# A selective-scan layer with a feed-forward network: ScalarE's side work moved behind the two decay exponentials of each group, and one exponential of the carried state issued two groups later

## The chip, the core and the metric

The kernel runs on one core of a Trainium2 chip. A core has five engines that work side by side, each through its own queue in order: TensorE (PE, matrix products, with PEld for its weight loads), VectorE (DVE), ScalarE (ACT), GpSimd (POOL) and SyncE (SP, which here only starts DMAs). An instruction that needs another engine's result waits on a semaphore, and everything behind it in its queue waits with it. The metric is the device time of one execution in microseconds (us); the three timed runs of the kernel before took 2914.01, 2914.90 and 2921.65 us, median 2914.9.

## What is computed

The input x is 2 sequences of 1024 tokens with 512 channels. The layer is a selective state-space model, a residual and a layer norm, then a gated feed-forward network, a residual and a layer norm:

```python
xn = x * rsqrt(mean(x*x) + 1e-6) * norm_w
xn = xn * sigmoid((xn @ select_proj_w.T + select_proj_b) * select_gate)
delta, B, C = split(xn @ x_proj_w.T)              # 128 + 128 + 128
dt = softplus(delta @ dt_proj_w.T + dt_proj_b)    # 512 channels
A = -exp(A_log)                                   # 512 x 128
h = exp(dt * A) * h + (dt * xn) * B               # per token: 512 x 128 states
y = sum over the 128 states of h * C
x = layernorm(x + (y + x * D) @ out_proj_w.T)
x = layernorm(x + (silu(x @ w_gate.T) * (x @ w_up.T)) @ w_down.T)   # 512 -> 2048 -> 512
```

The recurrence over tokens is the large part: 512 x 128 states for each of 2048 tokens.

## The kernel before

**Blocks, halves and groups.** The 2048 tokens are cut into 64 blocks of S = 32 tokens (`st`). A block is done in two halves (`h`, with `i` = 0 or 1), a half in eight groups (`r` = 0 to 7), so there are 1024 groups (`k`), 16 in a block. In this text the groups of a block are numbered 0 to 15; groups 0 to 7 have `i` = 0. A group covers 32 channels x 32 tokens with the 128 states on the partitions, and is one scan on VectorE over 1024 columns (L730): `h = a * h + bu`.

**The main path of a group.** TensorE makes `bu` = B (dt x) for the group with two matrix products (L709), and `a` = A dt for the *next* group with two more (L418). ScalarE turns those two into the decay factors `a_sb` with two exponentials (`decay_exp`, L425); this document calls the two the *pair* of the group. `a` has two buffers, so the next group's `a` products can only start when this group's pair has been read; `bu` has two buffers as well, and `a_sb` three. The state carried over from the previous block is added to the first column of `bu`: in even groups by VectorE (L727, from `cd`), in odd ones by a ScalarE copy of a sum made beforehand (L717, from `cu`). Groups 1, 5, 9 and 13 also run 16 products of the previous half's `h` with C (`y_round`, L437; the profile shows each product as two records, so 32).

**The carried state.** For each block, `load` fetches the first token's dt into all partitions (`cd`), the u rows (`cu`) and b0. At the end of group 5, `carry_a` for the next block issues three operations: ScalarE scales `cu` (L361), POOL multiplies `cd` by A (L362), and ScalarE takes the exponential of that product (L363). After group 9 of the same block, and after group 1 of the next, `carry_h` multiplies the result by the last states on POOL (L375, L376).

**The side work.** Everything else is written as Python generators that the class `Work` steps while the groups are issued: `pre` (norm, gate, projections, dt and u of the next 128 or 256 tokens), `post` (out projection, residual, norm), `ffn` and `silu`. A generator yields "E" when its next step is work for the other engines, "P" when it next wants TensorE and the one PSUM bank of the side work, and "H" while it holds that bank with products still to issue. `Work.others` steps each generator that stands at "E" once. `Work.tensor` issues one unit of products for the holder. `PARTS = (3, 0, 2, 3, 3, 0, 2, 3)` is what each group of a half adds to the credit of units; in groups with 0 no side products are issued.

**The order within a group, as issued:** first `others()` (L689, all side operations), then in group 0 `load` for the next block and in group 8 `y_out` of the previous block (ScalarE copies the finished `y` out of PSUM, L450, three POOL operations follow, L451 to L453), then the four products, the odd groups' copy (L717), the first exponential of the pair, VectorE's addition (L727), the second exponential, the scan, the C h products, the side products, `diag` (POOL builds the diagonal operands `ddt` and `du` of later groups, L389 and L399), and at last the carry operations. The order of calls is the order in each engine's queue.

**One chain of side work matters below.** A pair of feed-forward hidden tiles goes: products `gu` (L553) -> ScalarE copies them out (L561) -> POOL clamps and multiplies (L593, L594) -> ScalarE exp and ln (L596, L597) -> ScalarE exp (L599) -> POOL product into `hid` (L601). Four such pairs make half of `hid`; then the products `d` (L575) over its eight columns run, one unit for each column. Each arrow over "E" costs one call of `others()`. After `d`, VectorE adds the result to the row (L581).

Of the kernel before, what the change touches and what calls it, by code (L numbers as in the profile page):

```python
# [10 lines left out]
AF = mybir.ActivationFunctionType  # L11
# [10 lines left out]
PARTS = (3, 0, 2, 3, 3, 0, 2, 3)  # L22
# [12 lines left out]
def kernel(  # L35
# [17 lines left out]
    nc = tc.nc  # L53
# [11 lines left out]
    NSB = L // S  # L65
    NS = B * NSB
# [265 lines left out]
    prepared, carried, dus, ddts, hs, ys = {}, {}, {}, {}, {}, {}  # L332

    def load(st):


        ub = step_pool.tile([P, 2, P], FP, tag="ub", name=f"ub_{st}")
        nc.sync.dma_start(ub, ub_d[st].rearrange("g t b c -> (g t) b c"))
        prepared[st] = ub
        nc.gpsimd.tensor_copy(  # L340
            cz[st % 3][:, 28:284].rearrange("p (b w) -> p b w", w=32)[:, :, 0:4],
            made[lot_of[st]][1][:, toks(st)].rearrange("p (b t) -> p b t", t=4),
        )
        if st % NSB:
            cd = step_pool.tile([P, D], FP, tag="cd", name=f"cd_{st}")
            nc.sync.dma_start(cd, dt0_d[st : st + 1, :].to_broadcast([P, D]))
            cu = step_pool.tile([P, 2, P], FP, tag="cu", name=f"cu_{st}")
            for g in range(2):
                nc.sync.dma_start(
                    cu[:, g, :], ub_d[st, 2 + g, 0:1, 0, :].to_broadcast([P, P])  # L350
                )
            b0 = step_pool.tile([P, 1], FP, tag="b0", name=f"b0_{st}")
            nc.sync.dma_start(b0, ub_d[st, 0, 0, 1, :].unsqueeze(1))
            carried[st] = cd, cu, b0

    def carry_a(st):

        if st % NSB == 0:
            return
        cd, cu, b0 = carried[st]  # L360
        nc.scalar.activation(cu, cu, AF.Copy, scale=b0)  # L361
        nc.gpsimd.tensor_tensor(cd, a_n, cd, ALU.mult)  # L362
        nc.scalar.activation(cd, cd, AF.Exp, scale=-1.0)  # L363

    def carry_h(st, i):

# [41 lines left out]
    def place(k):  # L408
        h, r = divmod(k, 8)
        m, pair = divmod(r, 2)  # L410
        return h, m, pair

    def decay_mm(k, b):

        h, m, pair = place(k)
        g = 2 * pair + b
        ps = ps_a.tile([P, 16, S], FP, tag="a", name=f"a_{k}_{b}")
        nc.tensor.matmul(  # L418
            ps, a_t[ts(g, 32), m, :], ddts[k // 4][ts(g, 32), m % 2, :, :],
            start=True, stop=True,  # L420
        )
        return ps

    def decay_exp(k, b, ps):
        nc.scalar.activation(  # L425
            a_sb[:, k % 3, ts(b, 16), 1:], ps[:, :, 1:], AF.Exp, scale=-1.0
        )
# [16 lines left out]
    def y_out(st):  # L444

        tt, s = divmod(st, 4)
        if s == 0:
            yrs[tt] = post_pool.tile([P, 4, P], FP, tag="yr", name=f"yr_{tt}")
        yc = post_pool.tile([P, P, 4], FP, tag="yc", name=f"yc_{st}")
        nc.scalar.copy(yc, ys.pop(st).rearrange("p (q t) -> p q t", t=4))  # L450
        nc.gpsimd.tensor_tensor(yc, yc, pick.unsqueeze(1).to_broadcast([P, P, 4]), ALU.mult)  # L451
        nc.gpsimd.tensor_tensor(yc[:, :, 0:2], yc[:, :, 0:2], yc[:, :, 2:4], ALU.add)
        nc.gpsimd.tensor_tensor(yrs[tt][:, s, :], yc[:, :, 0], yc[:, :, 1], ALU.add)  # L453
        if s == 3:
            work.add(post(tt), front=True)
# [3 lines left out]
    def post(tt):  # L459

        zT = post_pool.tile([P, NM, P], FP, tag="zT", name=f"zT_{tt}")
        nc.sync.dma_start(zT, x_q.rearrange("(m p) t -> p m t", p=P)[:, :, ts(tt, P)])
        yield "E"
        yield "E"
        nc.gpsimd.tensor_tensor(zT, zT, dq.unsqueeze(2).to_broadcast([P, NM, P]), ALU.mult)
        yield "E"
        yield "P"
        ps = misc(f"zT_{tt}", 2)
        for s in range(4):
            nc.tensor.transpose(ps[:, ts(s, P)], yrs[tt][:, s, :], ident)  # L470
            if s == 1:
                yield "H"
        yield "E"
        z = zT.rearrange("p m (s t) -> p s m t", t=S)
        nc.vector.tensor_tensor(
            z, z, ps.rearrange("p (s m t) -> p s m t", m=NM, t=S), ALU.add
        )
        x1 = post_pool.tile([P, D], FP, tag="x1", name=f"x1_{tt}", bufs=4)
        nc.sync.dma_start(x1, xf[tt])
        yield "P"  # L480
        ps = misc(f"op_{tt}", 8)
        for half in (slice(0, 256), slice(256, 512)):
            for k in range(NM):
                nc.tensor.matmul(  # L484
                    ps[:, half], zT[:, k, :], out_w[:, k, half], start=(k == 0), stop=(k == NM - 1)
                )
                yield "H" if half.start == 0 or k + 1 < NM else "E"
        nc.vector.tensor_tensor(x1, x1, ps, ALU.add)
        yield "E"
        yield from normalize(x1, f"a{tt}")  # L490
        work.add(ffn(tt, x1))
# [129 lines left out]
    class Work:  # L621
# [11 lines left out]
        def step(self, item):  # L633
# [2 lines left out]
                self.gens.remove(item)  # L636
            item[1] = kind

        def others(self):
            for item in list(self.gens):  # L640
                if item[1] == "E":
                    if self.holder is item:
                        self.holder = None
                    self.step(item)
# [22 lines left out]
    work = Work()  # L667
# [17 lines left out]
    for k in range(NG):  # L685
        h, m, pair = place(k)
        st, i = divmod(h, 2)
        r = k % 8
        work.others()  # L689
        if r == 0:  # L690
            hs[h] = half_pool.tile([P, 256, S], FP, tag="h", name=f"h_{h}")

            if i == 1 and st:
                y_out(st - 1)
            if i == 0:
                c = lot_of[st]
                if c + 1 < NC and c not in begun:
                    begun.add(c)
                    pres[c + 1] = work.add(pre(c + 1), front=True)
                if st + 1 < NS:  # L700
                    if lot_of[st + 1] > c:
                        work.finish(pres[c + 1])
                    load(st + 1)

        bu = ps_bu.tile([P, 32, S], FP, tag="bu", name=f"bu_{k}")
        nxt = []
        for b in range(2):
            g = 2 * pair + b
            nc.tensor.matmul(  # L709
                bu[:, ts(b, 16), :], prepared[st][ts(g, 32), 1, :],  # L710
                dus[k // 4][ts(g, 32), m % 2, :, :],
                start=True, stop=True,
            )
            if k + 1 < NG:
                nxt.append(decay_mm(k + 1, b))
        if st % NSB and pair:
            nc.scalar.copy(  # L717
                bu[:, :, 0].rearrange("p (g e) -> p g e", e=16),
                carried[st][1][:, :, ts(2 * m + i, 16)],
            )  # L720
        if nxt:
            decay_exp(k + 1, 0, nxt[0])
        if st % NSB and not pair:
            left = carried[st][0].rearrange("p (b i e) -> p b i e", i=2, e=16)
            first = bu[:, :, 0].rearrange("p (b e) -> p b e", e=16)
            at = 4 * m + 2 * pair
            nc.vector.tensor_tensor(first, first, left[:, at : at + 2, i, :], ALU.add)  # L727
        if nxt:
            decay_exp(k + 1, 1, nxt[1])
        nc.vector.tensor_tensor_scan(  # L730
            hs[h][:, ts(r, 32), :].rearrange("p q t -> p (q t)"),
            a_sb[:, k % 3, :, :].rearrange("p q t -> p (q t)"),
            bu.rearrange("p q t -> p (q t)"),
            0.0, ALU.mult, ALU.add,
        )
        if h:
            for b in ROUNDS[r]:
                y_round(h - 1, b)
        credit = min(credit + PARTS[r], 6)
        done, most = 0, min(credit, 4)  # L740
        while PARTS[r] and (done < most or done < 4 and work.left == 1):

            if done == 3 and work.left == 2:
                break
            if not work.tensor():
                break
            done += 1
        credit -= done

        j, r4 = divmod(k, 4)  # L750
        if r4 == 3:
            diag(j + 2, 0)
        else:
            diag(j + 1, r4 + 1)
        if r == 1:
            if i == 0 and st:
                carry_h(st, 1)
            if i == 1 and st + 1 < NS:
                carry_h(st + 1, 0)
        if r == 5 and i == 0 and st + 1 < NS:  # L760
            carry_a(st + 1)
    for j in range(8):
        y_round(2 * NS - 1, j)
    y_out(NS - 1)
# [79 lines left out]
```

## Time and profile before

| | before |
|---|---|
| median of 3 runs | 2914.9 us |
| the profiled execution, whole | 2915.46 us |
| its span | 2913.5 us |
| PE busy | 2814.4 us |
| DVE busy | 2459.7 us (the 1024 scans: 2315.0) |
| POOL busy | 1837.0 us |
| ACT busy | 1640.5 us (the 2048 decay exponentials: 1084.1) |
| mean granted TensorE clock | 0.977 |
| first scan starts / last one ends | 43.7 / 2843.8 us |

Busy time is the union of an engine's records. A TensorE record begins when the product enters the array's queue, so a stretch in which the products wait on a semaphore is partly shown as busy, and a busy PE is not a PE at its peak. "Idle before" in the tables is the engine's idle time just before an instruction, and the arrow names what ended it. "PEclk" is the granted share of the TensorE clock. Of the whole time, about 41 us lie before the first group and 72 us behind the last one, where the last 128 tokens go through the feed-forward network alone; the 1024 groups between them take 2800 us, 2.73 us each.

### The profile page before, as it was taken

How to read it: one execution, taken by the hardware profiler on the slowest of the kernel's cores; microseconds unless marked ns; L12 is line 12 of the kernel's file. 1: busy time of each engine (PE TensorE's matmuls, PEld its weight loads, DVE VectorE, ACT ScalarE, POOL GpSimd, SP SyncE). 2: the span in 40 equal slices, each digit the busy share in tenths (PEclk: the TensorE clock that was granted, in tenths of full speed). 3: DMA queues.
4: the chain of work that ended last, by engine and by line, in shares of the span. 5: the costliest groups of instructions: out<-in, count | busy, mean ns of one | idle time of the engine just before them, and what ended most of it. 6: DMA issues, size and time to landing. Idle time of an engine off the chain costs nothing.

```text
span 2913.5 us, 58135 instructions
## 1 busy us (share of the span) xinstructions
PE 2814.4 (97%) x22728; PEld 1541.5 (53%) x22728; DVE 2459.7 (84%) x1680; ACT 1640.5 (56%) x3663; POOL 1837.0 (63%) x2140
## 2 busy tenths in 40 slices
PE   7989999999999999999999999999999999999998
PEld 4435555555555554555545555555555555455557
DVE  2998898888888988888888888989888898888881
ACT  4656566555565556655556555655556555455552
POOL 4656676666676666666567666566576666566653
PEclk6999999999999999999999999999999999999999
DMA  2011331323223331323313332133322323222325
GB/s 75 23 30 66 97 100 55 120 93 111 73 76 111 98 119 56 93 94 106 118 58 88 101 112 94 65 99 103 113 92 73 106 81 123 92 88 84 109 88 181
DMA packets 139166, 266.86 MB, mean 92 GB/s; under 512 B 22480, under 2 KB 76240, under 8 KB 138896
## 3 DMA queue, kind: packets, MB, share of 16 engines
q1 hardware_dynamic: 138896, 263.16, 28.1%
q8 instruction: 182, 2.98, 0.4%
q14 instruction: 88, 0.72, 0.1%
HBM read 250.39 MB, written 12.71 MB: 90 GB/s over the span
## 4 chain that ended last, share of the span: by engine, by line
PE 84%; DVE 6%; issue 3%; ACT 3%; POOL 3%; DMA 1%; SPq 0%; DVEq 0%; ACTq 0%; POOLq 0%
PE bu L709 30%; PE gu L553 18%; PE y L437 15%; PE d L575 8%; PE a L418 7%; DVE h L730 5%; PE sel L187 2%; PE op L484 2%; PE xp L187 1%; ACT a_sb L425 1%; POOL cd L362 1%; DMA ub_d<-uT 1%; PE b L251 1%; POOL du L399 1%; PE ss L204 0%
## 5 line engine op out<-in xcount | busy, mean ns | idle before, releaser
L730 DVE TENSOR_TENSOR_SCAN h<-a_sb,bu 128x1024 f32<-128x1024 f32 x1024 | 2315.0, 2280 | 233.5 <-ACT bu L717 120.7
L425 ACT ACTIVATE a_sb<-a 128x496 f32<-128x496 f32 x2048 | 1084.1, 582 | 590.5 <-PE a L418 545.2
L418 PE MATMUL a<-ddt,a_t 32*128 32x512 f32 x4096 | 1276.0, 652 | 15.6 <-ACT a_sb L425 12.8
L709 PE MATMUL bu<-du,ub 32*128 32x512 f32 x4096 | 1248.1, 650 | 20.7 <-DVE h L730 18.7
L389 POOL TENSOR_TENSOR ddt<-dt,hot 128x512 f32<-128x512 f32 x512 | 532.3, 1047 | 334.5 <-PE a L418 334.1
L553 PEld LDWEIGHTS gu<-x1T,w 128*128 128x128 f32 x4096 | 486.0, 192 | 275.4 <-issue 214.0
L553 PE MATMUL gu<-x1T,w 128*128 128x128 f32 x4096 | 551.8, 285 | 12.7 <-ACT t L315 5.1
L399 POOL TENSOR_TENSOR du<-ub,hot 128x512 f32<-128x512 f32 x512 | 534.5, 1048 | 17.8 <-PE a L418 12.7
L709 PEld LDWEIGHTS bu<-du,ub 32*128 32x128 f32 x4096 | 351.7, 186 | 330.4 <-issue 184.2
L437 PE MATMUL y<-h,cz 128*32 128x256 f32 x8192 | 502.0, 386 | 0.6 <-DVE h L730 0.6
L418 PEld LDWEIGHTS a<-ddt,a_t 32*128 32x128 f32 x4096 | 394.3, 187 | 70.0 <-issue 34.5
L437 PEld LDWEIGHTS y<-h,cz 128*32 128x32 f32 x8192 | 242.5, 110 | 334.4 <-issue 203.5
L717 ACT COPY bu<-cu 128x32 f32<-128x32 f32 x496 | 94.6, 191 | 451.0 <-PE a L418 249.7
L593 POOL TENSOR_SCALAR gu<-gu 128x256 f32<-128x256 f32 x128 | 108.2, 846 | 312.8 <-ACT gu L561 310.3
L575 PE MATMUL d<-w,hid 128*128 128x256 f32 x1024 | 268.0, 401 | 2.5 <-ACT t L315 2.3
L575 PEld LDWEIGHTS d<-w,hid 128*128 128x128 f32 x1024 | 185.2, 193 | 145.0 <-issue 94.1
L727 DVE TENSOR_TENSOR bu<-bu,cd 128x32 f32<-128x32 f32 x496 | 96.1, 194 | 155.7 <-PE a L418 142.8
L451 POOL TENSOR_TENSOR yc<-yc,pick 128x512 f32<-128x512 f32 x64 | 66.5, 1039 | 140.9 <-ACT yc L450 140.9
L601 POOL TENSOR_TENSOR hid<-gu,e 128x256 f32<-128x256 f32 x128 | 92.8, 725 | 78.3 <-ACT e L599 77.9
L375 POOL TENSOR_TENSOR cd<-cd,h 128x256 f32<-128x256 f32 x124 | 106.0, 855 | 38.4 <-DVE h L730 38.4
L561 ACT COPY gu<-gu 128x512 f32<-128x512 f32 x128 | 74.9, 585 | 59.5 <-PE gu L553 59.2
L594 POOL TENSOR_TENSOR gu<-gu 128x256 f32<-128x256 f32 x128 | 94.4, 737 | 10.7
(89 smaller groups left out, 1402.1 us busy)
## 6 DMA issues: line engine op xcount, KB each, us to landing
w<-in_wgu_s_dram SPq DMA_DIRECT2D x256, 512.0 KB, 3.8
w<-in_wd_s_dram SPq DMA_DIRECT2D x128, 512.0 KB, 3.6
cd<-dt_d SPq DMA_DIRECT2D x62, 256.0 KB, 3.5
ub<-ub_d SPq DMA_DIRECT2D x64, 128.0 KB, 2.0
cu<-ub_d SPq DMA_DIRECT2D x124, 64.0 KB, 4.9
ub_d<-bt SPq DMA_DIRECT2D x64, 64.0 KB, 1.8
ub_d<-uT SPq DMA_DIRECT2D x64, 64.0 KB, 1.8
zT<-in_x_q_dram SPq DMA_DIRECT2D x16, 256.0 KB, 7.0
```

Source lines behind the costliest of these rows:

```text
L375: nc.gpsimd.tensor_tensor(cd, cd, last, ALU.mult)
L389: nc.gpsimd.tensor_tensor(ddts[j][:, m, :, :], made[lot_of[st]][0][:, a + m, toks(st)].unsqueeze(1).to_broadcast([P, 16, S]), hot[:, ts(i, ...
L399: nc.gpsimd.tensor_tensor(dus[j][:, m, :, :], uv[:, a + m, :].unsqueeze(2).to_broadcast([P, 16, S]), hot.unsqueeze(1).to_broadcast([P, 16, ...
L418: nc.tensor.matmul(ps, a_t[ts(g, 32), m, :], ddts[k // 4][ts(g, 32), m % 2, :, :], start=True, stop=True,)
L425: nc.scalar.activation(a_sb[:, k % 3, ts(b, 16), 1:], ps[:, :, 1:], AF.Exp, scale=-1.0)
L437: nc.tensor.matmul(ys[st][ts(m, 32), ts(i, 256)], cz[st % 3][:, at : at + 32], hs[h][:, ts(m, 64), ts(b, 4)], start=(i == 0 and b == 0), s ...
L553: nc.tensor.matmul(ps[:, ts(2 * a + b, P)], w[:, a, k, :], x1T[:, k, :], start=(k == 0), stop=(k == NM - 1),)
L575: nc.tensor.matmul(ps[:, 0:HD], hid[:, f, :], w[:, f % 4, :], start=(f == 0), stop=(f == NH - 1),)
L593: nc.gpsimd.tensor_scalar_max(g, g, -80.0)
L709: nc.tensor.matmul(bu[:, ts(b, 16), :], prepared[st][ts(g, 32), 1, :], dus[k // 4][ts(g, 32), m % 2, :, :], start=True, stop=True,)
L727: nc.vector.tensor_tensor(first, first, left[:, at : at + 2, i, :], ALU.add)
L730: nc.vector.tensor_tensor_scan(hs[h][:, ts(r, 32), :].rearrange("p q t -> p (q t)"), a_sb[:, k % 3, :, :].rearrange("p q t -> p (q t)"), b ...
```

## The change

Three things move; no operation is added, removed or resized.

1. The exponential of `cd` leaves `carry_a` and becomes `carry_exp`, issued at the end of group 7 instead of group 5.
2. `others()` and `y_out` are issued behind the pair: the order in a group is now the four products, the odd groups' copy, both exponentials, then all side operations, then VectorE's addition and the scan. `load` stays ahead of the products, and so is now ahead of the side operations' DMAs in group 0.
3. One side operation stays ahead: in the six groups of a half that have side products (PARTS not 0), a new `give_back` first steps the generator that holds the side bank if it stands at "E", which is the step that empties the bank. In groups 1, 5, 9 and 13 that step too comes behind the pair.

```diff
         nc.gpsimd.tensor_tensor(cd, a_n, cd, ALU.mult)
-        nc.scalar.activation(cd, cd, AF.Exp, scale=-1.0)
+
+    def carry_exp(st):
+        if st % NSB:
+            cd = carried[st][0]
+            nc.scalar.activation(cd, cd, AF.Exp, scale=-1.0)
...
+        def give_back(self):
+
+            item = self.holder
+            if item is not None and item[1] == "E":
+                self.holder = None
+                self.step(item)
+
...
-        work.others()
+
+        if PARTS[r]:
+            work.give_back()
         if r == 0:
             hs[h] = half_pool.tile([P, 256, S], FP, tag="h", name=f"h_{h}")
-
-            if i == 1 and st:
-                y_out(st - 1)
...
         if nxt:
             decay_exp(k + 1, 0, nxt[0])
+        if nxt:
+            decay_exp(k + 1, 1, nxt[1])
+        work.others()
+
+        if r == 0 and i == 1 and st:
+            y_out(st - 1)
...
-        if nxt:
-            decay_exp(k + 1, 1, nxt[1])
...
         if r == 5 and i == 0 and st + 1 < NS:
             carry_a(st + 1)
+        if r == 7 and i == 0 and st + 1 < NS:
+            carry_exp(st + 1)
```

## The prediction

> **What bounds the kernel now.** I read the page first (busy shares, the chain), then the waits, then the stretches where groups are long, and last the program order.
>
> ```profile
> PE 2814.4 (97%) x22728; PEld 1541.5 (53%) x22728; DVE 2459.7 (84%) x1680; ACT 1640.5 (56%) x3663; POOL 1837.0 (63%) x2140
> PE 84%; DVE 6%; issue 3%; ACT 3%; POOL 3%; DMA 1%; SPq 0%; DVEq 0%; ACTq 0%; POOLq 0%
> ```
>
> TensorE carries the chain. But its records begin before a wait ends, so I took the time from one group's first `bu` product to the next group's, in the timeline. Undisturbed kinds are very regular: a group with 12 `gu` records 2.61 us (2.74 in odd places), with 8 records 2.16, with the 32 `y` records 2.94, with 8 `d` records 2.99. Sixteen such groups make a block of 41.8 us, and block 31 has that. The 64 blocks take 2800 us, 43.75 each. So about 2 us a block is lost somewhere, more in some blocks. In the waits view two lines show where ScalarE, which is only 56% busy, holds TensorE up:
>
> ```profile
> ACT cd L363 <- POOL cd L362: 37.9, 24, 2.0
> PEld a L418 <- ACT a_sb L425: 22.8, 75, 0.9
> ```
>
> The chain in block 30 around its group 7, columns start us, us, what, shows how:
>
> ```profile
> 1365.29 0.74 POOL gu L594
> 1366.03 1.01 POOL du L399
> 1367.04 1.23 POOL cd L362
> 1368.27 0.02 issue
> 1368.29 0.63 ACT cd L363
> 1368.92 0.32 ACT e L596
> 1369.24 0.02 issue
> 1369.26 0.02 ACT e L597
> 1369.28 0.39 issue
> 1369.68 0.57 ACT a_sb L425
> 1370.25 0.14 issue
> 1370.39 0.66 PE a L418
> ```
>
> POOL is late with `cd`, ScalarE stands 1.89 us at L363, two silu operations follow, and only then the pair, whose input was ready near 1367.7. The next group's `a` product waits until 1370.39: that group takes 4.68 us instead of 2.74. The same stall can cost more where TensorE had little to do before it (windows view: block 31 whole, then block 56 behind its group 6):
>
> ```profile
> 1396.00:1438.00 42.00, 42.00 (x366) 23.47 (x365) 38.21 (x27) 21.73 (x50) 23.21 (x27) 1.00 0.34 111
> 2502.00:2512.00 10.00, 8.13 (x24) 3.91 (x22) 4.67 (x3) 4.34 (x10) 6.77 (x9) 0.66 0.00 0
> ```
>
> The seventh figure is the granted clock: 0.66. There the eight `d` records take 3.71 us on the chain instead of 1.93.
>
> **Part 1, the exponential of cd moves from group 5 to group 7.** The operation stays (62 x 0.63 us); the wait goes, as L362 now has two more groups, some 4.5 us, against a worst lateness of 2.0. For every block in which L363 waited I compared the late group, and the one behind it, with the undisturbed time of its kind. Blocks 14, 22, 30, 32, 38, 48, 54: 1.97 us each, 13.8. Blocks 59 and 61: 3.1 together. Blocks 11 and 19: 2.2 together. Blocks 16, 24, 40, 46, with the clock at half for one window: 3.6 each, 14.4. Blocks 13, 56, 58, where group 6 had no side products and the clock fell for two windows: 14.3. Sum 47.8 us. Without the clock's share it would be 16 x 1.95 + 2.2 = 33; these are the ends, and I take 48, since the clock records fall just there.
>
> The Trainium skill, "TensorE: Matmul & The Clock Gate", Part 1, says that the clock halves after an idle window of about 3.4 us. In blocks 16, 24, 40 and 46 it fell at a stall near 2 us, so the rule as stated would give Part 1 only the 33; the trace decides.
>
> In its new place the 0.63 us lies between the pairs of groups 7 and 8. In the program's order it is joined there in a block by at most an L322 (1.15) and a copy (0.58); that is counted in Part 2.
>
> **Part 2, side operations behind the pair.** The built order decides here. In block 28, groups 0 to 14, ScalarE's list *between two pairs* is the same before and after but for cd and the copy of y: before it runs copy, pair, exp and ln, pair, exp, pair; after it runs copy (now by `give_back`), pair, exp and ln, pair, exp, pair. What stood "ahead of the next pair" now stands "behind this one", the same place in a queue. So the pairs come no earlier by it. I added the mean durations listed between each two pairs and compared them with the time that TensorE's next `a` product leaves (1.1 to 1.7 us by the kind of group): 56 groups are overfull by 17.6 us in all before, 51 by 17.6 after. Cost 0; the ends are -18 (none of it costs anything) and +18 (it doubles).
>
> What does move is TensorE's side work: a generator needs one group fewer from bank to next product. The groups without any side product are 78 before, 75 after; what is left behind the last group is the same (128 `gu`, 37 `d`, 8 `op` products). Counting every group from block 4 on at its kind's time, and at no less than the 2.26 us that a product, its pair and the next product need, gives 2538 before and 2537 after: 0. Two pairs of adjacent empty groups in blocks 27 and 51, with a half clock (6.36 and 6.44 us for a `y` group that takes 2.94), are no longer adjacent, but blocks 56 and 60 have 4 and 8 empty groups where they had 1 and 5. I take -6; ends -12 and +8.
>
> **Part 3, what now comes later.** (a) The copy of `y` (0.59) in group 8 is behind the pair, behind exp and ln of a silu in seven blocks, and the `y` products of group 9 need that bank: by their places 0.2 to 0.5 us late in some nine blocks, +3. POOL's three products behind it (1.04, 0.61, 0.42) start some 2.5 us later and `diag` is queued behind them; `du` of group 12 has about 0.8 us left by my count, so I put +5, ends 0 and +40 (the rival below). (b) The copies of u and of the first dt wait for a DMA to free their row:
>
> ```profile
> ACT t L315 <- DMA ub_d<-uT: 18.3, 8, 3.2
> ACT uT L292 <- DMA ub_d<-uT: 4.9, 4, 2.1
> ```
>
> They empty the bank, so they stay ahead of the pair. In four chunks of tokens the first copy now falls behind a pair, which leaves its DMA a group less: 3.4 us where it was 1.5 to 3.8; in three chunks the last copy is behind a pair, 2.1 where it was 2.2 to 3.4. Together +3; ends -4, +8. (c) In three blocks the square L197 (1.06) comes behind exp and ln after an empty group, and `ss` waits about 1 us: +3. (d) VectorE's side operations L581 or L488 (0.40, 0.66) and the statistics (0.86) now fall in one group ahead of a scan, 30 times, most of it inside VectorE's slack of 0.25 us a group: +4, ends 0 and +8. (e) SP: the five DMAs of `load` are now ahead of the weight fetches of group 0. The first waits for the block before to release `ub`, at most the length of one group; a piece is fetched four ahead (over 5 us), so 0. If a fetch came late, one group in a block would wait for part of its 3.8 us.
>
> One fear I could drop from a row. `d` now starts in the group whose side operations, behind the pair, finish the last `hid` columns, in 12 of 30 starts. If `d` waited for the whole tile, TensorE would stand some 2.4 us each time, 29 us. Block 37 shows that it does not: the `d` products (first row) begin before POOL writes the last columns (second row), and only the seventh unit, one group later, reads those.
>
> ```profile
> 1671.81 1.99 PE L575 MATMUL d<-w,hid 128*128 128x256 f32 x8
> ...
> 1672.32 0.73 POOL L601 TENSOR_TENSOR hid<-gu,e 128x256 f32<-128x256 f32 x1 [1.11 <-ACT e L599]
> ```
>
> **Sum.** -48 - 6 + 3 + 5 + 3 + 3 + 4 = -36. The profiled execution took 2915.5 us (span 2913.5 and 2.0 around it), 0.6 over the median of the runs: 2915.5 - 36 = 2879.5, so 2879.
>
> **Rivals.** *A new wait through POOL, slower.* Side steps on POOL that follow a ScalarE step of the same group (L601 behind L599, L451 behind L450, L593 where the copy is behind the pair) now wait for the pair first, up to 2.3 us, with `diag` and `cd` queued behind them. If `du` or `ddt` come late for `bu` or `a`, TensorE stands. Against: POOL is 63% busy, and a `diag` has three groups before it is needed. For: a wait of POOL for `ACT yc` is already 140.9 us. At 0.8 us of TensorE in each of 62 blocks beyond my +5 (50 us) it ends at 2929; it decides from 0.6 us a block (2915).
> *The wait comes back.* POOL is so much later that L363 waits at group 7 too, or its 0.63 us delays the pair of group 8 in most blocks: half of the 48 lost and 62 x 0.2 = 12 us added gives 2915, no change. Against: a worst lateness of 2.0 us and two groups gained.
> *The pairs do come earlier.* If my claim that the queue is the same fails in favour of the change, the overfull 17.6 us and the double empties (another 6) vanish: 2855.
>
> **How the numbers follow.** My forecast 0.55, the pairs earlier 0.14, the wait comes back 0.11, slower through POOL 0.20. A difference under 0.3% (8.7 us) can't be told from none in this kernel. Of the forecast's spread, from 2855 to 2906, nearly all is faster: faster 0.70, same 0.11, slower 0.19. From the ends of the parts, -48-18-12-4 = -82 and -33+18+8+3+5+8+3+8 = +20 would be 2833 and 2936; all at once is unlikely, and the +40 of Part 3 (a) is the rival. The range 2845 to 2924 leaves out 0.05 below and about 0.15 above; the forecast's own range is 2855 to 2906.
>
> **What would show it.** Right: the waits have no L363 <- L362 line; group 7 of block 30 and its like take 2.7 us; fewer stretches with the clock at half; the 75 short waits of `a` for a pair (22.8 us) stay in the main, since the pairs come no earlier elsewhere. Wrong: waits of `bu` for POOL `du`, now 12.3 us, in the tens; a wait of `y` for the copy of y, now not in the list; `d` waiting for POOL `hid`; blocks such as 31 over 41.8 us.

## The result and the profile after

The changed kernel is slower. Its median over 20 runs is 2926.12 us (2919.0 to 2934.46) against 2913.8 us for the kernel before over 20 runs (2908.71 to 2921.65); the ratio is 1.0042, with a 95% interval of 1.0032 to 1.0052. The forecast was 2879 us, faster, and its range ended at 2924. The profiled execution took 2923.86 us, its span is 2922.0.

The lines below are from the page of the kernel after: the engines' busy times, and the shares of the chain that ended last.

```profile
PE 2798.2 (96%) x22728; PEld 1528.1 (52%) x22728; DVE 2463.5 (84%) x1680; ACT 1634.2 (56%) x3663; POOL 1837.0 (63%) x2140
...
PE 80%; DVE 8%; ACT 4%; POOL 4%; issue 3%; DMA 1%; SPq 0%; DVEq 0%; POOLq 0%; ACTq 0%
```

Every engine executes the same number of instructions as before and POOL has the same busy time to a tenth of a microsecond. What changed is the chain: TensorE carries 80% of it where it carried 84%, and VectorE, ScalarE and POOL carry 16% where they carried 12%. Work was not added; waits were.

The waits view gives engine and line, releaser: us in all, times, longest. First the kernel before, four lines that the readings below need:

```profile
PE a L418 <- ACT a_sb L425: 12.8, 15, 1.9
...
ACT e L596 <- POOL gu L593: 10.4, 11, 1.3
...
PE op L484 <- DVE zT L475: 4.7, 4, 1.4
...
ACT x L500 <- POOL off_f L499: 1.7, 2, 1.3
```

The kernel after:

```profile
POOL yc L455 <- ACT yc L454: 198.9, 55, 16.4
...
POOL hid L605 <- ACT e L603: 124.7, 99, 3.0
...
PEld y L441 <- ACT yc L454: 34.5, 42, 1.1
ACT e L600 <- POOL gu L597: 34.0, 29, 4.1
...
PEld a L422 <- ACT a_sb L429: 27.4, 67, 2.8
...
ACT x L504 <- POOL off_f L503: 21.0, 12, 4.2
...
ACT t L315 <- DMA ub_d<-uT: 15.3, 7, 4.4
...
PEld bu L719 <- POOL du L403: 14.3, 36, 1.1
...
PE uT L287 <- POOL u L280: 10.5, 5, 5.5
...
PE op L488 <- DVE zT L479: 9.7, 9, 2.0
...
PE a L422 <- ACT a_sb L429: 4.5, 3, 1.9
```

The wait of 37.9 us at the exponential of `cd` is gone. In the same view of the kernel before, the silu exponential had waited 10.4 us for POOL (now 34.0), the layer norm's last step 1.7 us (now 21.0), POOL's product into `hid` 77.9 us (now 124.7), and POOL's first product on `y` 140.9 us (now 198.9); the wait of the `y` products for the copy of `y` was not in the list. The wait of `bu` for POOL's `du` moved from 12.3 to 14.3 only.

Of these rows, TensorE's own tell most about the time. Its products `a`, which need the pair, wait for it less than before: 4.5 us in 3 places, where it was 12.8 in 15. Its products of the side work (all but `bu`, `a` and `y`) wait more. Added up over the loop of the 1024 groups, their waits for another engine of over 0.15 us are 60.7 us in 76 places, where the kernel before has 29.7 in 45.

Where the time went is read from the group lengths of the prediction's first part. I call a group late when it is 0.5 us or more over the time of its kind, and add up what the late groups lose by their number in the block:

| group of the block | 7 | 8 | 9 | 0 | 1 | 3 | 11 | 12 | time at half clock |
|---|---|---|---|---|---|---|---|---|---|
| before, us | 60.5 | 21.9 | 18.3 | 17.6 | 6.4 | 21.9 | 8.2 | 9.5 | 58.0 |
| after, us | 9.7 | 11.3 | 9.3 | 32.1 | 15.4 | 28.8 | 26.1 | 45.3 | 71.7 |

(The clock's column takes the record of the granted clock from 217 us to 75 us before the end.) Group 7 gave back 51 us, as forecast. Groups 0, 1, 3, 11 and 12 lose 84 us more than before, group 12 most. The other eight groups, left out of the table, lose about as much in all as before. From the first scan to the end of the last the loop took 2800 us before and 2810 after.

Two late groups show what happens there. The first is group 12 of block 33, 8.24 us long where the undisturbed kind takes 2.61. First ScalarE's timeline (start us, us, engine, line, operation, and in brackets the idle time before and what ended it):

```profile
1502.04 1.06 ACT L429 ACTIVATE a_sb<-a 128x496 f32<-128x496 f32 x2 [1.14 <-PE a L422]
1507.33 0.81 ACT L504 ACTIVATE x<-x,off_f,rstd_f 128x512 f32<-128x512 f32 x1 [4.23 <-POOL off_f L503]
1508.05 0.17 ACT L727 COPY bu<-cu 128x32 f32<-128x32 f32 x1
1508.16 1.05 ACT L429 ACTIVATE a_sb<-a 128x496 f32<-128x496 f32 x2
```

And POOL's timeline of the same stretch:

```profile
1499.00 1.04 POOL L455 TENSOR_TENSOR yc<-yc,pick 128x512 f32<-128x512 f32 x1 [3.98 <-ACT yc L454]
1500.12 0.62 POOL L456 TENSOR_TENSOR yc<-yc 128x256 f32<-128x256 f32 x1
1500.82 0.42 POOL L457 TENSOR_TENSOR yr<-yc 128x128 f32<-128x128 f32 x1
1501.19 1.05 POOL L393 TENSOR_TENSOR ddt<-dt,hot 128x512 f32<-128x512 f32 x1
1502.20 1.27 POOL L237 TENSOR_TENSOR xT<-xT,dt 128x512 f32<-128x512 f32 x1
1503.42 1.05 POOL L403 TENSOR_TENSOR du<-ub,hot 128x512 f32<-128x512 f32 x1
1504.42 0.88 POOL L379 TENSOR_TENSOR cd<-cd,h 128x256 f32<-128x256 f32 x1
1505.38 0.45 POOL L380 TENSOR_TENSOR cu<-cu,cd 128x128 f32<-128x128 f32 x1
1505.79 1.26 POOL L237 TENSOR_TENSOR xT<-xT,dt 128x512 f32<-128x512 f32 x1
1507.03 0.27 POOL L503 TENSOR_SCALAR off_f<-mv_f,rstd_f 128x1 f32<-128x1 f32 x1
```

POOL stood 3.98 us for the copy of `y`, then worked 8.3 us with no gap over 0.1 us. The 0.27 us of L503 was the last in that queue. ScalarE came to L504, which needs it, at 1503.1 and stood until 1507.3. Behind L504 in ScalarE's queue are the copy L727 and the pair, and TensorE's `a` product waits for the pair: its `bu` products ended at 1506.86 and the next `a` product ran at 1508.79. Then the clock, in the windows view of the kernel after (bounds, length, busy time and records of PE, PEld, DVE, ACT and POOL, granted clock, DMA share, GB/s):

```profile
1500.00:1505.70 5.70, 5.70 (x56) 3.40 (x44) 4.38 (x3) 1.93 (x6) 5.47 (x8) 1.00 0.00 0
...
1509.00:1516.00 7.00, 7.00 (x27) 3.60 (x25) 3.93 (x3) 1.38 (x3) 1.31 (x2) 0.53 0.56 187
```

After a stop of 1.93 us the granted clock is 0.53 over the next 7 us. The Trainium skill, "TensorE: Matmul & The Clock Gate", Part 1, gives an idle window of about 3.4 us as the condition; this trace again shows the fall after a shorter stop, as the prediction had found in the kernel before.

Such groups cost much, but they are few: the `a` products stood for the pair in blocks 33, 41 and 56 alone, each time behind L504. These three groups 12 lose 15.9 us, their half clock included.

The second is group 12 of block 44, 4.59 us long where its kind takes 2.99 (rows of VectorE, ScalarE and TensorE, by start):

```profile
2007.65 0.66 DVE L479 TENSOR_TENSOR zT<-zT,zT 128x512 f32<-128x512 f32 x1
...
2008.05 0.42 ACT L600 ACTIVATE e<-gu 128x256 f32<-128x256 f32 x1 [1.75 <-POOL gu L597]
...
2008.36 1.99 PE L488 MATMUL op<-out_w,zT 128*128 128x256 f32 x8 [0.89 <-DVE zT L479]
```

Here TensorE itself stands. The out projection's products `op` are asked for before VectorE has added to `zT`, which it does behind a scan that ends at 2007.7. ScalarE waits in the same group, 1.75 us for POOL's `gu`, but that wait ends 0.3 us before TensorE's. In eight blocks the `op` products of group 12 wait so (in the kernel before, three groups of the loop have it); in blocks 34 and 42 group 12 holds transposes of `u` that wait for POOL's product L280. All late groups from block 4 on in which a side product waits over 0.3 us lose 82 us, against 37 in the kernel before and 42 with part 1 alone. So most of the loss lies where TensorE's own side products come too early, and less of it behind ScalarE.

### The profile page after: what moved, and what is told of

It reads as the page before. It is cut to its first block, busy times and chain, and to the rows that moved or that the text cites. A ratio compares the mean times of both kernels' runs of the same rounds, so it can differ in the third digit from the quotient of the medians.

```text
span 2922.0 us, 58263 instructions
## 1 busy us (share of the span) xinstructions
PE 2798.2 (96%) x22728; PEld 1528.1 (52%) x22728; DVE 2463.5 (84%) x1680; ACT 1634.2 (56%) x3663; POOL 1837.0 (63%) x2140
## 4 chain that ended last, share of the span: by engine, by line
PE 80%; DVE 8%; ACT 4%; POOL 4%; issue 3%; DMA 1%; SPq 0%; DVEq 0%; POOLq 0%; ACTq 0%
PE bu L719 29%; PE gu L557 16%; PE y L441 15%; PE d L579 7%; DVE h L744 7%; PE a L422 5%; PE sel L187 2%; PE op L488 1%; ACT a_sb L429 1%; PE xp L187 1%; DMA ub_d<-uT 1%; PE b L251 1%; POOL ddt L393 1%; POOL du L403 0%; POOL dt L325 0%
## 5 line engine op out<-in xcount | busy, mean ns | idle before, releaser
L719 PE MATMUL bu<-du,ub 32*128 32x512 f32 x4096 | 1233.4, 650 | 20.4 <-DVE h L744 18.0
L557 PE MATMUL gu<-x1T,w 128*128 128x128 f32 x4096 | 552.0, 285 | 12.8 <-ACT t L315 4.6
L422 PEld LDWEIGHTS a<-ddt,a_t 32*128 32x128 f32 x4096 | 389.8, 186 | 50.2 <-ACT a_sb L429 27.4
L727 ACT COPY bu<-cu 128x32 f32<-128x32 f32 x496 | 93.9, 189 | 508.9 <-PE a L422 330.3
L455 POOL TENSOR_TENSOR yc<-yc,pick 128x512 f32<-128x512 f32 x64 | 66.7, 1043 | 198.9 <-ACT yc L454 198.9
L605 POOL TENSOR_TENSOR hid<-gu,e 128x256 f32<-128x256 f32 x128 | 93.0, 726 | 125.3 <-ACT e L603 124.7
```

Of the source, the lines that this page charges most:

```text
L422: nc.tensor.matmul(ps, a_t[ts(g, 32), m, :], ddts[k // 4][ts(g, 32), m % 2, :, :], start=True, stop=True,)
L557: nc.tensor.matmul(ps[:, ts(2 * a + b, P)], w[:, a, k, :], x1T[:, k, :], start=(k == 0), stop=(k == NM - 1),)
L719: nc.tensor.matmul(bu[:, ts(b, 16), :], prepared[st][ts(g, 32), 1, :], dus[k // 4][ts(g, 32), m % 2, :, :], start=True, stop=True,)
```

## The experiments

Each kernel is compared with the kernel before on the same chip. Differences between two changed kernels are of medians that were partly taken on different chips; where they are small, the two ratios are the better guide. The first question was which of the parts costs the time; the second, through which wait; the third, where the gain of the first part goes.

### Part 1 alone

The kernel before, with the exponential of `cd` moved to group 7 and nothing else.

```diff
-        nc.scalar.activation(cd, cd, AF.Exp, scale=-1.0)
+    def carry_exp(st):
+        if st % NSB:
+            cd = carried[st][0]
+            nc.scalar.activation(cd, cd, AF.Exp, scale=-1.0)
...
+        if r == 7 and i == 0 and st + 1 < NS:
+            carry_exp(st + 1)
```

> The kernel before with the first part of the change alone: the exponential of cd issued at the end of group 7, everything else where it was. Theory A (the parts oppose each other: the removed wait was worth what the prediction said, and moving side work behind the pair cost more): 2866 us, 48 under before. Theory B (the wait was never worth that, because what waits for POOL there would have waited somewhere else): 2905 to 2914, within 10 of before.

Measured: 2884.64 us against 2909.87, ratio 0.9901 (0.9862 to 0.9939), 25 us faster. The wait for `cd` is gone; late groups 7 lose 17.0 us instead of 60.5, and the blocks named in the prediction gained 45.5 us. So the mechanism and size of the first part hold in their place. But some 20 us came back in the profiled execution: 8 in blocks 27, 35, 43 and 51, each with a stretch at half clock close by, 3 in group 8 of five other blocks, 7 in the first four blocks and the rest in blocks 6 to 9. From first `bu` to first `bu`, group 9 of blocks 35 and 43 takes 6.0 and 7.0 us where the kernel before has 3.9; in blocks 27 and 51 it was late before (6.4) and takes 7.0. This is taken up below.

### Parts 2 and 3 alone

The kernel after, with the exponential of `cd` back at group 5.

```diff
         nc.gpsimd.tensor_tensor(cd, a_n, cd, ALU.mult)
+        nc.scalar.activation(cd, cd, AF.Exp, scale=-1.0)
...
-        if r == 7 and i == 0 and st + 1 < NS:
-            carry_exp(st + 1)
```

> The changed kernel with the exponential of cd back at group 5: the second part of the change alone. Theory A: before + 60 = 2974 us, or less if side work behind the pair happens to leave ScalarE free at group 5. Theory B: within 10 us of the changed kernel's 2926.

Measured: 2996.05 us, ratio 1.0283 (1.0246 to 1.032): the side operations and the copy of `y` behind the pair cost 86 us by themselves. The waits view of this kernel (its lines are one further on than in the kernel after):

```profile
ACT cd L363 <- POOL cd L362: 74.4, 31, 4.4
...
ACT e L601 <- POOL gu L598: 32.3, 27, 3.9
```

The waits for the silu and the norm (20.9 us) are those of the kernel after, and the wait for `cd` has doubled, from 37.9 to 74.4 us: POOL's answer comes later there too. TensorE's side products wait 57.8 us in the loop, nearly as in the kernel after; with part 1 alone it is 32.4. The time at half clock is 122.9 us. So the parts don't add: the first is worth 25 us on the kernel before and 70 us (2996 - 2926) on top of the second, which makes the wait that the first removes twice as long.

### The copy of y

Two kernels: the kernel after with `y_out` back ahead of the products, and the kernel with part 1 alone with `y_out` behind the pair.

```diff
+            if i == 1 and st:
+                y_out(st - 1)
...
-        if r == 0 and i == 1 and st:
-            y_out(st - 1)
```

> The changed kernel with y_out of group 8 back ahead of the products, all else as changed. Theory C (POOL's backlog after group 8, from the product with the copy of y that now waits for the pair, is what the later ScalarE operations wait for): the excess of groups 9 to 13 goes, some 35 to 50 us less, 2880 to 2890. Theory D (the cause is that a side step and the next one now fall in one group, so that ScalarE waits for POOL's answer wherever POOL is busy): 0 to 12 us less, 2914 to 2926.

> The kernel before with the exponential of cd at group 7 and y_out behind the pair, the other side operations ahead as before. Theory C: 35 to 50 us over the run with the exponential alone. Theory D: 0 to 12 us over it.

Measured: 2918.24 us (ratio 1.0027, 1.001 to 1.0044), 8 us less than the kernel after, and 2891.41 us (0.9934, 0.9907 to 0.9961), 7 us more than part 1 alone. By the ratios the differences are some 4 and 10 us. Both point the same way, but each interval overlaps that of the kernel it is compared with: the later copy of `y` costs 4 to 10 us, or nothing. In the first, group 12 loses 24.4 us instead of 45.3, but group 11 loses 37.3 instead of 26.1: half of what leaves one group turns up in the one ahead of it. The larger part of the loss has another cause. The second kernel also shows how little a wait of ScalarE for POOL can cost: its silu exponentials wait 41.7 us, where part 1 alone has 11.5.

### diag ahead of the side operations

The kernel after, with `diag` issued ahead of `others()`, so that POOL's `ddt` and `du` no longer queue behind a product that waits for ScalarE.

```diff
+        j, r4 = divmod(k, 4)
+        if r4 == 3:
+            diag(j + 2, 0)
+        else:
+            diag(j + 1, r4 + 1)
         work.others()
...
-        j, r4 = divmod(k, 4)
-        if r4 == 3:
-            diag(j + 2, 0)
-        else:
-            diag(j + 1, r4 + 1)
```

> The changed kernel with the call of diag moved ahead of others(), so that POOL builds its diagonal operand before the side operations that wait for a ScalarE result of the same group. Theory E (POOL stands at the head of its queue for results that now come behind the pair, L605 124.7 us and L455 198.9 us, and what it does next is late for ScalarE): 25 to 40 us less than the changed kernel, 2886 to 2900, and the waits of ScalarE for POOL (L600 34.0, L504 21.0) under 25 together. Theory F (POOL's own order does not matter; side steps are simply one step too early for any answer): within 10 us of 2926.

Measured: 2920.47 us, ratio 1.0026 (1.001 to 1.0041), 6 us less than the kernel after. The waits view of this kernel:

```profile
POOL hid L605 <- ACT e L603: 73.6, 86, 2.1
...
ACT e L600 <- POOL gu L597: 24.2, 22, 4.1
...
ACT x L504 <- POOL off_f L503: 20.9, 12, 4.3
```

POOL's wait for the silu fell to below that of the kernel before (77.9), and the time hardly moved. So neither that wait nor `ddt` and `du` behind it are the main cause. ScalarE's wait for the norm stayed, and so did the waits of TensorE's side products (61.6 us). The interval overlaps that of the kernel after (1.0032 to 1.0052), so 6 us is near the limit of what can be told; the rival's mechanism, as the prediction put it, is worth no more than that.

### One step between POOL's offset and the norm that needs it

The kernel after, with one more "E" between L503 and L504, so that ScalarE comes to the norm a group later.

```diff
         nc.gpsimd.tensor_scalar(off, mv[:, 0:1], rstd, -1.0, ALU.mult, ALU.mult)
+        yield "E"
         nc.scalar.activation(t, t, AF.Identity, bias=off, scale=rstd)
```

> The changed kernel with one more yield between POOL's offset of a layer norm (L503) and ScalarE's use of it (L504), so that ScalarE reaches it a group later. Both theories: the 21.0 us of ScalarE's wait go, with the groups of 8.2 and 7.3 us in blocks 33 and 41 and their half clock: 15 to 25 us less, 2901 to 2911. If it moves less than 8 us, those waits were covered by others.

Measured: 2905.3 us, ratio 0.9964 (0.9948 to 0.9979), 21 us less than the kernel after. The waits view of this kernel (lines one further on from L504):

```profile
ACT e L601 <- POOL gu L598: 30.4, 27, 4.1
...
ACT x L505 <- POOL off_f L503: 5.5, 5, 1.9
```

The 21.0 us of this wait went to 5.5, and the kernel is 21 us faster; the time at half clock went from 71.7 to 34.1 us. The wait of TensorE's `a` products for the pair (4.5 us) is gone, and its side products wait as before the edit (60.3). So this run separates the two kinds of late groups: the norm's wait is worth some 20 us, about half of what parts 2 and 3 cost on top of part 1. The price is not exact, since the added step shifts the later side work too: blocks 33 and 41, with the norm, are 5.9 and 6.9 us shorter, but so is block 34, where TensorE had stood for POOL's `u`, by 6.6.

### At most one step of a generator in a group

In the kernel after, a generator can be stepped twice in one group: `give_back` takes its copy out of the bank ahead of the pair, and `others()`, behind the pair, takes its next step, for which POOL has only the length of a pair. This kernel steps each generator once a group at most.

```diff
+        due = list(work.gens)
         if PARTS[r]:
+            held = work.holder
             work.give_back()
+            if work.holder is not held:
+                due = [x for x in due if x is not held]
...
-        work.others()
+        work.others(due)
```

> The changed kernel with each generator stepped at most once in a group: what give_back stepped, or added, is left out of others() of that group. 46 of 128 silu exponentials then come two pairs behind their copy instead of one; empty groups 78 instead of 75. Theory F: the wait of L600 for POOL goes (34.0 to under 12), 20 to 35 us less, 2891 to 2906. Theory E: POOL still stands for L603 and L454, the gain is under 12 us, 2914 to 2926.

Measured: 2883.39 us, ratio 0.9896 (0.9863 to 0.9928), 43 us less than the kernel after, and the same as part 1 alone (0.9901). The waits view of this kernel:

```profile
POOL hid L605 <- ACT e L603: 98.4, 66, 3.9
...
ACT e L600 <- POOL gu L597: 8.4, 9, 1.0
```

The silu's wait is 8.4 us, below the 10.4 of the kernel before, and the norm's wait is back at 1.7 us; the time at half clock is 23.9 us. TensorE's side products wait 46.4 us in the loop instead of 60.7, and its `a` products no longer wait for the pair. In the program's order, 46 of the 128 silu exponentials now stand two pairs behind the copy that they depend on, where in the kernel before and in the kernel after 120 stand one pair behind it and 8 none. All the other side operations are still behind the pair, and POOL still waits more than in the kernel before. So the place behind the pair costs nothing measurable by itself; what costs is that a step is reached before the other engine has answered the one ahead of it, by ScalarE or by TensorE. The edit lowers both kinds of waits at once. It also changes how fast the side work goes through the groups (78 groups without side products, as before, where the kernel after has 75), and no run separates these.

### The bank emptied first in every group

The kernel after, with `give_back` in the groups without side products too.

```diff
-        if PARTS[r]:
-            work.give_back()
+        work.give_back()
```

> The changed kernel with give_back in every group, so that the side bank is emptied ahead of the pair in groups 1, 5, 9 and 13 too. 62 groups without side products instead of 75. If the step behind the pair in those four groups is what costs (POOL waits for the copy from there on): 15 to 30 us less, 2896 to 2911. If not: within 8 us of 2926.

Measured: 2901.44 us, ratio 0.996 (0.9945 to 0.9975), 25 us less than the kernel after. The groups without side products fall from 75 to 62, but the silu waits 49.1 us for POOL, longer than in the kernel after. TensorE's side products wait 48.4 us, less than in the kernel after. These are two effects of opposite sign; how large each is stays open. The run does show that the total of ScalarE's waits does not order these kernels.

### Where part 1's gain came back, and the row of u

In the kernel with part 1 alone, ScalarE's timeline around group 8 of block 35:

```profile
1581.19 1.05 ACT L429 ACTIVATE a_sb<-a 128x496 f32<-128x496 f32 x2
1582.13 0.63 ACT L367 ACTIVATE cd<-cd 128x512 f32<-128x512 f32 x1
1582.65 0.42 ACT L600 ACTIVATE e<-gu 128x256 f32<-128x256 f32 x1
1583.10 0.51 ACT L601 ACTIVATE e<-e,ones 128x256 f32<-128x256 f32 x1
1583.52 0.56 ACT L454 COPY yc<-y 128x512 f32<-128x512 f32 x1
1583.98 1.06 ACT L429 ACTIVATE a_sb<-a 128x496 f32<-128x496 f32 x2
```

Between one pair and the next ScalarE has 2.1 us of work without a gap, 0.63 of it the moved exponential. In the kernel before the same stretch held the other three alone, and the next pair began 2.27 us after the last one instead of 2.79. Four kernels follow: the exponential at group 6 (`r == 6` in place of `r == 7`), a second buffer for the row through which u and the first dt go to memory (the waits of ScalarE for that row's DMA are 18.3 and 4.9 us in the kernel before), both together, and the second buffer on the kernel with one step a group.

```diff
-            t = pre_pool.tile([P, D], FP, tag="row", name=f"uT_{c}_{j}")
+            t = pre_pool.tile([P, D], FP, tag="row", name=f"uT_{c}_{j}", bufs=2)
...
-        t = pre_pool.tile([P, D], FP, tag="row", name=f"t0_{c}")
+        t = pre_pool.tile([P, D], FP, tag="row", name=f"t0_{c}", bufs=2)
```

> The kernel before with the exponential of cd alone moved, to group 6 instead of group 7. With the move to group 7 alone, the blocks in which ScalarE had stood for cd gave 45 us, but about 20 came back elsewhere: group 9 of blocks 27, 35, 43, 51 (3 to 4 us each, with the clock at half) and group 8 of blocks 18, 26, 34, 42, 50 (0.5 each). Theory G, the place: there the 0.63 us stands ahead of two silu operations and the copy of y, between the pairs issued in groups 7 and 8, where ScalarE has no room. One group earlier ScalarE has only the copy of gu beside it, and L362 still has one group (2.2 us or more) against a worst lateness of 2.0 us: about 2870 us, y in group 9 of block 35 back from 5.1 to 3.9 us or less, waits for cd under 5 us. Theory H, any move shifts ScalarE against POOL and the time comes back somewhere: 2880 to 2890. Rival, the wait comes back since one group is not enough: waits for cd over 10 us and over 2890.

> The exponential of cd at group 7 alone, and two buffers instead of one for the row that carries u and the first dt to memory, so that their copies no longer wait for the DMA of the row before. In the profile of that move alone those waits are 18.0 us at the copy of dt (8 times) and about 5 at the copies of u, all on ScalarE ahead of a pair. Theory: they stop the pair, so most of it comes off the end: 2865 to 2872 us, and no line of a DMA for t or uT in the list of waits. Rival: TensorE has work meanwhile, and the time stays within 4 us of 2885.

> The changed kernel with at most one step of a side generator in a group, and two buffers for the row. One step alone took 2883. Theory: the waits for the row's DMA come off as in the kernel with the exponential alone, 2865 to 2872 us; the order of the side operations then makes no difference, within 5 us of that kernel with two rows. Rival: 2883 again, if the steps behind the pair had hidden these waits.

> The kernel before with the exponential of cd at group 6 and two buffers for the row. If both places are separate stalls of ScalarE ahead of a pair, their gains add: about 2855 us (15 for the place, 15 for the row, off 2885). If the place is not the cause (theory H) it equals the kernel with two rows and the exponential at group 7, 2865 to 2872.

Measured, all against 2915.82 us for the kernel before:

| kernel | median, us | ratio, 95% interval |
|---|---|---|
| exponential at group 6 | 2867.13 | 0.9835 (0.9798 to 0.9872) |
| at group 7, two rows | 2862.75 | 0.9817 (0.9787 to 0.9846) |
| one step a group, two rows | 2852.09 | 0.9786 (0.9753 to 0.9818) |
| at group 6, two rows | 2846.25 | 0.9777 (0.9734 to 0.982) |

*The place.* At group 6 the exponential lies beside the copy of `gu` alone, in a group in which ScalarE waits for TensorE anyway. The same stretch of block 35 in that kernel's timeline of ScalarE:

```profile
1561.85 1.06 ACT L429 ACTIVATE a_sb<-a 128x496 f32<-128x496 f32 x2 [1.31 <-PE a L422]
1562.80 0.63 ACT L367 ACTIVATE cd<-cd 128x512 f32<-128x512 f32 x1
1563.81 0.59 ACT L565 COPY gu<-gu 128x512 f32<-128x512 f32 x1 [0.38 <-PE gu L557]
1564.95 0.19 ACT L721 COPY bu<-cu 128x32 f32<-128x32 f32 x1 [0.55 <-PE a L422]
1565.07 1.05 ACT L429 ACTIVATE a_sb<-a 128x496 f32<-128x496 f32 x2
```

Idle gaps of 0.38 and 0.55 us are left on both sides of the copy: the 0.63 us fits. From its scan to the next one, group 9 of blocks 35, 43 and 51 takes 3.1 us where it took 5.1, 5.4 and 5.8 with the exponential at group 7 (3.1, 3.1 and 6.3 in the kernel before); in block 27 it stays at 5.5. The gain over the kernel before is 49 us, what the prediction had put on the first part; in the profiled execution 47 us of it lie in the blocks that the prediction names. No wait for `cd` is left, so one group was enough for L362.

*The row.* The two lines of waits for the row's DMA are gone, 23 us of them, and with the exponential at group 7 the kernel is 22 us faster. Part of that is again the clock (37.5 us at half clock without the second row, 13.7 with it).

*Both.* The gains add: 18 for the place (2885 to 2867) and 22 for the row (2885 to 2863) off 2885 would give 2845, and it is 2846. The intervals of the last three rows overlap, so their order is not settled; that all are faster than the kernel before, by 1.5% or more at the ends of their intervals, is. In the profiled execution of the last one TensorE is closest to its full clock (0.977 in the kernel before):

```profile
core 0: 2844.8 us, clock 0.988
```

And one step a group with two rows, at 2852, is no slower than the kernel that leaves the side operations ahead of the pair: with the other engines' time to answer kept, the order of the side operations makes no measurable difference.

## Why the prediction was wrong

**Part 1 (-48): right in mechanism, place and size.** Group 7 gave 51 us in the kernel after, and the line of waits went. Alone at group 7 it is worth 25 us and not 48, in part since its 0.63 us meets silu operations and the copy of `y` there; one group earlier it is worth 49. In the kernel after that loss does not appear: groups 8 and 9 lost less than before, and the prediction's "at most an L322 and a copy" was said of that order.

**Part 2 (0 for the pairs, -6 for the side work): the step that failed.** For the pairs, the prediction took ScalarE's list between two pairs from the program's order, found it the same before and after, and concluded "the same place in a queue", cost 0, at most 18 us either way. For the side work, it counted every group at its kind's time (2538 against 2537) and added a gain. List and count are right; both leave out how long another engine has to answer. Parts 2 and 3 cost 86 us alone and 41 on top of part 1 (2926 against 2885), of which the copy of `y` explains 10 at most. Two waits showed in place of the 0 and the -6.

- *ScalarE for POOL, at the norm.* By the program's order, POOL's own operations that wait for ScalarE (L605, L455) now wait for a pair as well, and those behind them in POOL's queue, L503 among them, answer later (block 33 shows it behind L455). ScalarE meets L504 at the same place in its list and stands. That is shown: the run that gave POOL a group more for it took 21 us off.
- *TensorE for the inputs of its side products.* "A generator needs one group fewer from bank to next product" also means one group less for VectorE, ScalarE or POOL to make that product's input. These products wait 60.7 us in the loop where part 1 alone has 32.4, and the late groups that hold such a wait lose 40 us more. This is read from the traces: the two runs that lower these waits, one step a group (46.4 us) and the bank emptied first (48.4), change other waits too; they took 43 and 25 us off. How the 41 us divide between the two kinds stays open.

Of ScalarE's waits for POOL the silu's grew most (10.4 to 34.0 us), but it is not the main cost: with part 1 and the copy of `y` alone behind the pair it is 30 us longer than with part 1 alone, for 7 to 10 us of time.

**What held of the -6.** The count of 75 empty groups against 78 held, and the two places that the prediction named gave it: group 9 of blocks 27 and 51 takes 2.94 us where it took 6.36 and 6.44. Emptying the bank first everywhere, with 62 such groups, took 25 us off the kernel after; it was not isolated.

**Part 3 (a) (+5, ends 0 and +40) and the rival through POOL.** The rival put the time at 2929 and the result is 2926, but not by the rival's mechanism. It had `du` and `ddt` late for `bu` and `a`; the wait of `bu` for `du` rose by 2 us, and `diag` issued first took 5 or 6 us off. What held of it is its beginning, "side steps on POOL that follow a ScalarE step of the same group now wait for the pair first". What it missed is who waits next: at the norm ScalarE, with the copy, the pair and TensorE behind it, and more often TensorE's side products. The later copy of `y` was put at +3; two runs put it at 4 to 10, neither clear of the noise.

**Part 3 (b) (+3).** The waits for the row's DMA did not grow in all (18.3 to 15.3 us at the copy of the first dt, 4.9 to 6.2 at the copies of u), but one of them, 4.4 us in block 51, held TensorE's `d` products for 3.9. The prediction took them as they stand; the runs with a second row show that they cost about all they last (22 us for 23 of waiting, with part 1 in place).

**The fear that was dropped** stayed away: the list of waits has none of `d` for `hid`. The block taken as the undisturbed one, 31, takes 41.7 us (42.1 in the kernel before, a little over the 41.8 that the prediction read there), and the short waits of `a` for a pair stayed in the main (67 of them, 27.4 us, where there were 75 with 22.8), both as forecast.

**Part 3 (c) and (d) (+3, +4)** were not isolated by any run. The three waits of `ss` that (c) names are there, in blocks 24, 32 and 40, 0.67 us of TensorE each.

**The clock.** The prediction counted half-clock time as something that part 1 takes away. It can be lost after a stop near 2 us, and the kernel after made new ones: 71.7 us at half clock instead of 58.0.

## What to carry to other kernels

When operations move in one engine's queue, follow each chain through the other engine and back: count how long its answer has between the instruction that asks for it and the one that needs it, with what is queued ahead of it there. An unchanged list on the engine that stands proves nothing. Do the same for the bottleneck's own work: a product that is asked for earlier gains nothing if its input isn't there. The length of a wait is not its price: 15.5 us less at the norm went with 21 us less time, 30 us more at the silu with 7 to 10 us more. Look in each late group for the wait that ends last. If a scheduler steps a chain of work, let no chain take two steps in a slot that the other engine can't answer in; and put a moved operation into a slot where its engine still has idle gaps.

## What the runs showed of the hardware

The granted clock fell to a half after stops of TensorE near 2 us (1.93 us in block 33). Between the first 217 us, in which longer ones occur, and the last 75, these stretches last 3.4, 6.8 or 10.2 us and no others in all fourteen traces. Not every stop of that length is followed by one: in the kernel before, blocks 14 and 30 lost 1.97 us at the wait for `cd` with the clock at full, and blocks 16 and 24 some 3.6 us with the clock at half. Nor does it need such a stop: with part 1 alone the clock is at 0.50 from 1585.7 to 1589.1 us, in block 35, behind two groups without side products, and the longest idle time of TensorE recorded in that block's groups 7 to 9 is 0.22 us (its records begin before a wait ends). The time at half clock went from 58.0 us to 37.5 with part 1 alone, to 13.7 in the best kernel, and to 122.9 with parts 2 and 3 alone.
